# Expert layer of a cross-attention kernel: first tiles from three batches' tokens, routing of the fourth among the tiles, tiles past the 20th in branches

## The chip, the cores and the metric

One core of one Trainium2 chip runs the whole program as a single launch. The metric is device time in microseconds: the median over runs. The engines named below are PE (TensorE, matmuls), DVE (VectorE), ACT (ScalarE), POOL (GpSimd) and SP (SyncE, which only issues DMAs). Lines L... are those of the kernel before, unless the text says otherwise.

## The reference, cut to what matters

The input `x` is 4 batches x 512 tokens x 256 features, 2,048 tokens in all. Four layers follow each other, each adding to `x`:

```
def _L1_ffn_ref(x, W1, b1, W2, b2, Wr, br):          # D=256, H=1024, E=8, TOPK=2
    xf = x.reshape(-1, D)
    logits = xf @ Wr + br
    topv, _ = lax.top_k(logits, TOPK)
    masked = jnp.where(logits >= topv[:, 1:2], logits, -jnp.inf)
    weights = jax.nn.softmax(masked, axis=-1)
    h = gelu(jnp.einsum('td,edh->eth', xf, W1) + b1[:, None, :], approximate=False)
    expert_out = jnp.einsum('eth,ehd->etd', h, W2) + b2[:, None, :]
    return jnp.einsum('etd,te->td', expert_out, weights).reshape(B, S, D)

x = x + L0_xattn(...); x = x + L0_ffn(layernorm(x), ...)
x = x + L1_xattn(ctx, layernorm(x), ...); x = x + L1_ffn(layernorm(x), ...)
```

The last line's last term is the second expert layer, which the change is about. A token goes to the two experts with the largest logits, and to more only where logits tie. So 2,048 tokens make 4,096 rows of work, spread over eight experts as the router's choices fall. No expert has a capacity in this layer.

## The kernel before

The program runs four stages: attention 0 (to about 1710 us), the first expert layer (to about 1900), attention 1 (to 2676) and the second expert layer (to the end).

**How a token finds its expert.** The tensor `rows_x` in device memory has 2,048 places for each of the eight experts, 256 spare rows at the end, and in each row the 256 normalised features, the token's number and its eight routing weights (265 floats, 1,060 bytes). `clear_rows` (L334 to L345) fills it early in attention 0 with zeros and an out-of-range token number, by 32 DMAs of 530 KB and one of 265 KB on SP's queue. The exchanges of attention 0 (`swapped<-attn`, L700) are issued on SP behind them, and some on ACT.

`route2(b, ...)` (L347 to L473) routes a batch's tokens, in steps (it is a generator). It normalises four tiles of 128 tokens into `pay` (L354) and writes the token numbers behind them (L362); transposes them and multiplies by the router's matrix (L372); takes two experts by the two largest logits (L394 to L416); counts how many earlier tokens went to each expert (matmuls L432, L435) and so has each token's place; and scatters the rows of `pay` to those places with eight indirect DMAs on POOL (L446: four tiles, two experts). All of them write `rows_x`, so each waits for the one before. It ends by adding the second layer's bias to `x` (L459 to L470) and writing `x` to the output. `out` then holds everything but the expert products, which the tiles add to it.

**Where routing is done.** Attention 1 is a hand-written schedule in steps: for each batch four units (two halves of the features `o`, two halves of the tokens `f`) of 13 steps. `put(step, ...)` places a piece of work in a step, `spread` places a generator's pieces. Batch b-1 is routed during batch b (L1230: eight pieces, one per step). For batch 3 the units run with `f` outermost (L1034), so that the first half of its tokens is done after two units and is routed in the last two (L1251, L1252). The second half is routed after attention, ahead of the tiles (L1312). Within each engine the framework's planner places the instructions; it may move one ahead where its operands allow.

**The tiles.** From the counts a table (L1319 to L1362) is computed: expert by expert, as many tiles of 256 rows as its tokens fill; which expert's weights (`w_idx`) and which rows (`x_idx`) belong to tile i. There are always NG = 23 tiles (L52), the most that 4,096 rows over eight experts can need. A tile past the last real one reads the spare rows, whose token number is out of range, so its result is dropped. For tile i `fetch(i)` (L1364) gathers two blocks of 128 rows (L1368) and the expert's 2.1 MB of weights (L1378), by three indirect DMAs on POOL; `turned` (L1388) transposes the rows on PE (L1394) and copies them (L1395); `told` reads the token numbers and weights; `hidden` (L1409) is 32 matmuls (L1417 with gelu on ACT at L1425); `second` (L1433) is 32 more (L1436); `results` (L1495) multiplies by the routing weight on DVE (L1499) and adds to `out` by an accumulating scatter on POOL (L1500). Tile i+2 is fetched while tile i is computed, and the second product of tile i comes after the first of tile i+1. Row buffers are threefold, weights fourfold, results fivefold (`three`, `four`, `five`).

For ties a branch (L1457) computes the extra experts' share; its condition is loaded into a register, and it isn't taken where no logits tie.

Of the kernel before, what the change touches and what calls it, by code (L numbers as in the profile page):

```python
# [8 lines left out]
F32 = mybir.dt.float32  # L9
I32 = mybir.dt.int32  # L10
# [37 lines left out]

T = B * S
G = 256  # L50
GR = G // P
NG = (2 * T + E * (G - 1)) // G  # L52
ROWS = E * T
# [11 lines left out]
def xattn_ffn_twice(ctx: ExitStack, tc: tile.TileContext, a: dict, out: bass.AP):  # L65
# [79 lines left out]
    rows_x = dram.tile([ROWS + G, PAY], F32, name="rows_x")  # L145
# [176 lines left out]
    place2 = [const.tile([P, NX], I32, name=f"place2{k}") for k in range(2)]  # L322
# [11 lines left out]
    def clear_rows(empty):  # L334

        nc.gpsimd.memset(empty, 0.0)
        nc.gpsimd.memset(empty[:, :, D : D + 1], NOWHERE)
        n = ROWS // (4 * P)
        for i in range(n):
            nc.sync.dma_start(  # L340
                rows_x[i * 4 * P : (i + 1) * 4 * P, :].rearrange("(p r) d -> p r d", p=P), empty
            )
        nc.sync.dma_start(
            rows_x[ROWS:, :].rearrange("(p r) d -> p r d", p=P), empty[:, :GR, :]
        )  # L345

    def route2(b, two, psum, tag, first=0, n=NT):  # L347
# [90 lines left out]
        yield  # L438
        for k in range(2):
            off, place, at = small("off2"), wide("place"), place2[k][:, mine_b]  # L440
            nc.vector.tensor_tensor(place, hot[k], ps, ALU.mult)
            nc.vector.tensor_reduce(off, place, AX.X, ALU.add)
            nc.vector.scalar_tensor_tensor(off, chosen[k], float(T), off, ALU.mult, ALU.add)
            nc.vector.tensor_copy(at, off)
            for t in range(n):
                nc.gpsimd.indirect_dma_start(  # L446
                    out=rows_x[:, :],
                    out_offset=bass.IndirectOffsetOnAxis(ap=at[:, t : t + 1], axis=0),
                    in_=pay[:, t, :],
                    in_offset=None,  # L450
                    bounds_check=ROWS - 1,
                    oob_is_err=False,
                )

# [536 lines left out]
    with ExitStack() as st:  # L991
# [40 lines left out]
        for b in range(B):  # L1032
            order = [(o, f) for o in range(DC) for f in range(2)]
            if b == B - 1:  # L1034
                order = [(o, f) for f in range(2) for o in range(DC)]
            units += [(b, o, f) for o, f in order]
# [188 lines left out]
        for b in range(B):  # L1225
            s0 = per_batch * b
            if b:
                put(s0 - 10, lambda b=b: load_keys(b, 0))
                put(s0, lambda b=b: load_keys(b, 1))
                spread(s0 + 12, route2(b - 1, one, ps_s, "s"))  # L1230
# [20 lines left out]
        last_half = route2(B - 1, one, ps_s, "s", 0, NT // 2)  # L1251
        spread(per_batch * (B - 1) + 2 * NM + 12, last_half, 1, 8)  # L1252
# [49 lines left out]
    with ExitStack() as st:  # L1302
# [9 lines left out]
        for _ in route2(B - 1, two, ps_t, "t", NT // 2, NT // 2):  # L1312
            pass


        def bc(t, shape, at):
            return t.unsqueeze(at).to_broadcast(shape)

        count = one.tile([P, E], F32, name="count")  # L1319
        ps = ps_t.tile([P, E], F32, tag="t", name="ps_n")  # L1320
        nc.tensor.matmul(ps, lhsT=ones, rhs=taken2, start=True, stop=True)
        nc.vector.tensor_copy(count, ps)
        steps = one.tile([P, E, T // G], F32, name="steps")
        nc.vector.tensor_tensor(
            steps, bc(count, [P, E, T // G], 2), bc(full, [P, E, T // G], 1), ALU.is_gt
        )
        tiles = one.tile([P, E], F32, name="tiles")
        nc.vector.tensor_reduce(tiles, steps, AX.X, ALU.add)
        upto = one.tile([P, E], F32, name="upto")
        sums = one.tile([P, E, E], F32, name="sums")  # L1330
        nc.vector.tensor_tensor(sums, bc(tiles, [P, E, E], 1), notafter, ALU.mult)
        nc.vector.tensor_reduce(upto, sums, AX.X, ALU.add)
        past = one.tile([P, NG, E], F32, name="past")
        nc.vector.tensor_tensor(
            past, bc(number, [P, NG, E], 2), bc(upto, [P, NG, E], 1), ALU.is_ge
        )
        which = one.tile([P, NG], F32, name="which")
        nc.vector.tensor_reduce(which, past, AX.X, ALU.add)
        w_at = one.tile([P, NG], F32, name="w_at")
        w_idx = one.tile([P, NG], I32, name="w_idx")  # L1340
        nc.vector.tensor_scalar(w_at, which, float(E - 1), float(P), ALU.min, ALU.mult)
        nc.vector.tensor_scalar(w_at, w_at, lane[:, 0:1], None, ALU.add)
        nc.vector.tensor_copy(w_idx, w_at)

        spent = one.tile([P, NG, E], F32, name="spent")
        nc.vector.tensor_tensor(spent, past, bc(tiles, [P, NG, E], 1), ALU.mult)
        x_at = one.tile([P, NG], F32, name="x_at")
        nc.vector.tensor_reduce(x_at, spent, AX.X, ALU.add)
        nc.vector.tensor_tensor(x_at, number, x_at, ALU.subtract)
        held_ = one.tile([P, NG], F32, name="held_")  # L1350
        nc.vector.tensor_scalar(held_, which, float(E), None, ALU.is_lt)
        nc.vector.tensor_tensor(x_at, x_at, held_, ALU.mult)
        nc.vector.scalar_tensor_tensor(x_at, which, float(T // G), x_at, ALU.mult, ALU.add)
        nc.vector.tensor_scalar(x_at, x_at, float(G), lane[:, 0:1], ALU.mult, ALU.add)
        x_idx = one.tile([P, GR, NG], I32, name="x_idx")
        nc.vector.tensor_copy(x_idx[:, 0, :], x_at)
        for r in range(1, GR):
            nc.vector.tensor_scalar(x_at, x_at, float(P), None, ALU.add)
            nc.vector.tensor_copy(x_idx[:, r, :], x_at)
        mine = one.tile([P, NG, E], F32, name="mine2")  # L1360
        nc.vector.tensor_scalar(mine, past, -1.0, 1.0, ALU.mult, ALU.add)
        nc.vector.tensor_tensor(mine[:, :, 1:], mine[:, :, 1:], past[:, :, : E - 1], ALU.mult)  # L1362

        def fetch(i):  # L1364
            rows = []
            for r in range(GR):
                got = three.tile([P, PAY], F32, tag=f"rows{r}", name=f"rows{r}")
                nc.gpsimd.indirect_dma_start(  # L1368
                    out=got,
                    out_offset=None,  # L1370
                    in_=rows_x[:, :],
                    in_offset=bass.IndirectOffsetOnAxis(ap=x_idx[:, r, i : i + 1], axis=0),
                    bounds_check=ROWS + G - 1,
                    oob_is_err=False,
                )
                rows.append(got)
            w = four.tile([P, WIDE], F32, tag="w", name="w_e")
            nc.gpsimd.indirect_dma_start(  # L1378
                out=w,
                out_offset=None,  # L1380
                in_=a["wall"],
                in_offset=bass.IndirectOffsetOnAxis(ap=w_idx[:, i : i + 1], axis=0),
                bounds_check=E * P - 1,
                oob_is_err=False,
            )
            return w, rows
# [10 lines left out]

        def told(i, rows):

            to = five.tile([P, GR], I32, tag="to", name="to")  # L1400
            share = five.tile([P, GR], F32, tag="share", name="share")
            for r in range(GR):
                nc.vector.tensor_copy(to[:, r : r + 1], rows[r][:, D : D + 1])
                of = two.tile([P, E], F32, tag="told", name="told")
                nc.vector.tensor_tensor(of, rows[r][:, D + 1 :], mine[:, i, :], ALU.mult)
                nc.vector.tensor_reduce(share[:, r : r + 1], of, AX.X, ALU.add)
            return to, share
# [37 lines left out]
        fetched = [fetch(0), fetch(1)]  # L1445
# [3 lines left out]
        ps = ps_t.tile([P, NX], F32, tag="t", name="ps_x")  # L1449
        nc.tensor.matmul(ps, lhsT=ones, rhs=over, start=True, stop=True)  # L1450
        n_over = one.tile([P, 1], F32, name="n_over")
        nc.vector.tensor_reduce(n_over, ps, AX.X, ALU.add)
        n_over_i = one.tile([P, 1], I32, name="n_over_i")
        nc.vector.tensor_copy(n_over_i, n_over)
        ties = nc.values_load(n_over_i[0:1, 0:1], min_val=0, max_val=E * T)
        spare = st.enter_context(tc.tile_pool(name="d_spare", bufs=1))
        with tc.If(ties > 0):  # L1457
            for b in range(B):
                for t0 in range(0, NT, GR):
                    rows = []  # L1460
                    for r in range(GR):
                        j = b * NT + t0 + r
                        got = spare.tile([P, PAY], F32, tag=f"again{r}", name=f"again{r}")
                        nc.gpsimd.indirect_dma_start(
                            out=got,
                            out_offset=None,
                            in_=rows_x[:, :],
                            in_offset=bass.IndirectOffsetOnAxis(
                                ap=place2[0][:, j : j + 1], axis=0
                            ),  # L1470
                            bounds_check=ROWS + G - 1,
# [120 lines left out]
```

## Time and profile before

| what | us |
|---|---|
| median of 3 runs (3060.4 to 3063.5) | 3061.97 |
| the profiled execution | 3062.4 |
| its span, first to last instruction | 3060.7 |
| last update of `x` by attention 1 ends | 2676.7 |
| first hidden matmul of the tiles (L1417) | 2724.95 |
| last matmul of the tiles (L1436) ends | 3054.26 |
| last add to `out` issued (L1500) | 3055.09 |
| PE busy in the span | 2826.6 (92%) |
| mean granted clock of PE | 0.957 |

The span is what the profile shows; the execution's own time lies 1.7 us above it. In groups of instructions, a line reads: line, engine, operation, output<-input, shape, count, then busy time. In the timeline a line begins with the start and the duration, and a bracket at its end tells how long the engine was idle before and what released it. In a table of waits the numbers are total, times, longest. A cell of the windows is an engine's busy time with the number of its instructions.

### The profile page before, as it was taken

The page shows a single profiled execution, that of the slowest core. Times are in us where ns is not written, and L with a number is a line of the kernel's source. Part 1 is how long each engine was busy: PE and PEld are TensorE (multiplying, and loading weights), DVE is VectorE, ACT ScalarE, POOL GpSimd, SP SyncE. Part 2 cuts the span into 40 slices and gives each one's busy share as a digit, 9 for nine tenths or more (in the row PEclk, how much of TensorE's full clock was granted, in tenths as well). Part 3 has the DMA queues.
Part 4 walks back from the last instruction along what each step waited for, and adds up shares of the span by engine and source line. Part 5 has one row for each costly group of instructions (what it writes and reads, how often), then busy time and mean ns, then how long its engine had stood idle before and what let it go on. Part 6 is the DMA issues. An engine that isn't in the chain of part 4 may idle for free. (4 is left out here: it accounts for less than half of the span.)

```text
span 3060.7 us, 35871 instructions
## 1 busy us (share of the span) xinstructions
PE 2826.6 (92%) x13564; PEld 1885.8 (62%) x13564; DVE 1439.2 (47%) x2351; ACT 931.6 (30%) x1328; POOL 476.8 (16%) x347
## 2 busy tenths in 40 slices
PE   5899999999999999999997999599989897759999
PEld 2566666666666667676664666344545444448888
DVE  4365456544565444454443000577657566621111
ACT  2233234223342323323221211144334343412221
POOL 1000000100001000010001000333333333434442
PEclk9899999999999999999997999699999998969999
DMA  8543343343433433343333331300010100045562
GB/s 309 173 116 99 100 109 89 102 103 100 110 89 104 102 91 94 86 107 98 96 96 120 120 110 55 85 12 23 17 43 15 34 15 24 12 162 184 171 194 72
DMA packets 160942, 293.94 MB, mean 96 GB/s; under 512 B 42825, under 2 KB 78015, under 8 KB 157561
## 3 DMA queue, kind: packets, MB, share of 16 engines
q1 hardware_dynamic: 118280, 181.12, 21.3%
q0 software_dynamic: 17904, 74.77, 7.7%
q10 hardware_dynamic: 24576, 35.68, 4.5%
q8 instruction: 108, 1.77, 0.2%
q14 instruction: 74, 0.60, 0.1%
HBM read 100.24 MB, written 42.69 MB: 47 GB/s over the span
## 5 line engine op out<-in xcount | busy, mean ns | idle before, releaser
L687 DVE TENSOR_REDUCE top<-ps_s 128x1 f32<-128x2113 f32 x128 | 301.8, 2358 | 582.2 <-PE ps_s L679 576.6
L716 PE MATMUL ps_o<-pT,v 128*128 128x256 f32 x2176 | 521.6, 382 | 7.9 <-DVE pT L708 7.9
L679 PE MATMUL ps_s<-kT,qT 128*128 128x512 f32 (+1 forms) x1280 | 490.8, 528 | 15.2 <-ACT attn L693 14.7
L716 PEld LDWEIGHTS ps_o<-pT,v 128*128 128x128 f32 x2176 | 411.5, 192 | 125.1 <-issue 69.9
L679 PEld LDWEIGHTS ps_s<-kT,qT 128*128 128x128 f32 x1280 | 242.6, 191 | 265.7 <-issue 240.8
L693 ACT ACTIVATE attn<-ps_s,top 128x2113 f32<-128x2113 f32 x128 | 258.9, 2023 | 475.7 <-DVE top L687 411.2
L708 DVE STREAM_TRANSPOSE pT<-swapped 128x2176 f32<-128x2176 f32 x128 | 312.4, 2440 | 58.1 <-DMA swapped<-attn 48.2
L1080 DVE TENSOR_REDUCE tops<-ps_s 128x2 f32<-128x800 f32 (+1 forms) x256 | 243.0, 982 | 84.8 <-PE ps_s L1072 84.4
L1119 PE MATMUL ps_w<-asked,keyed 64*128 64x256 f32 (+1 forms) x1664 | 241.6, 422 | 41.0 <-DVE tops L1080 38.9
L629 PE MATMUL ps_k<-kvin,wkv 128*128 128x512 f32 (+1 forms) x640 | 262.1, 534 | 4.2 <-ACT kT L636 4.2
L1141 POOL TENSOR_TENSOR sum<-sum,pT 128x1024 f32<-128x1024 f32 x80 | 201.0, 2513 | 390.6 <-PE ps_o L1150 201.3
L662 PE MATMUL ps_v<-wkv,kvin 128*128 128x256 f32 x1088 | 253.5, 381 | 0.0
L1132 ACT ACTIVATE pT<-ps_w 128x1024 f32<-128x1024 f32 (+1 forms) x176 | 176.1, 1023 | 221.5 <-PE ps_w L1119 219.7
L1119 PEld LDWEIGHTS ps_w<-asked,keyed 64*128 64x128 f32 (+1 forms) x1664 | 156.0, 196 | 134.2 <-DVE tops L1080 74.4
L662 PEld LDWEIGHTS ps_v<-wkv,kvin 128*128 128x128 f32 x1088 | 204.9, 190 | 32.6 <-issue 3.3
L1072 PE MATMUL ps_s<-kT,qT 32*128 32x400 f32 (+1 forms) x1024 | 162.1, 588 | 30.1 <-DVE tops L1080 27.9
L1141 DVE TENSOR_TENSOR sum<-sum,pT 128x1024 f32<-128x1024 f32 x96 | 144.0, 1500 | 91.2 <-ACT pT L1132 78.0
L636 ACT ACTIVATE kT<-ps_k,bqk 128x512 f32<-128x512 f32 (+1 forms) x160 | 97.2, 620 | 268.2 <-PE ps_k L629 121.0
L629 PEld LDWEIGHTS ps_k<-kvin,wkv 128*128 128x128 f32 x640 | 116.5, 192 | 80.0 <-issue 67.1
L1417 PE MATMUL ps_h<-xT,w_e 128*128 128x256 f32 x736 | 164.7, 383 | 0.0
L1436 PE MATMUL ps_y<-w_e,hT 128*128 128x256 f32 x736 | 162.5, 379 | 0.0
L1417 PEld LDWEIGHTS ps_h<-xT,w_e 128*128 128x128 f32 x736 | 141.4, 192 | 19.6
(239 smaller groups left out, 2599.2 us busy)
## 6 DMA issues: line engine op xcount, KB each, us to landing
swapped<-attn SPq DMA_DIRECT2D x1536, 68.0 KB
swapped<-attn ACTq DMA_DIRECT2D x512, 68.0 KB
rows_x<-empty SPq DMA_DIRECT2D x32, 530.0 KB
w<-in_w_dram SPq DMA_DIRECT2D x16, 1024.0 KB
cT<-in_ctxT_dram SPq DMA_DIRECT2D x4, 1601.0 KB
keyed<-kT SPq DMA_DIRECT2D x32, 200.1 KB
ctx_b<-in_ctx_dram SPq DMA_DIRECT2D x4, 1536.0 KB
slot_x<-empty POOLq DMA_DIRECT2D x8, 512.0 KB
```

Source lines behind the costliest of these rows:

```text
L629: nc.tensor.matmul(ps[:, :n], lhsT=wkv[:, c, hs], rhs=flat_kvin[c][:, j0 : j0 + n], start=c == 0, stop=c == DC - 1,)
L662: nc.tensor.matmul(ps[:, k, :], lhsT=flat_kvin[c][:, j * P : (j + 1) * P], rhs=wkv[:, c, cols], start=c == 0, stop=c == DC - 1,)
L679: nc.tensor.matmul(flat[:, j0 : j0 + n], lhsT=qT[:, t * P : (t + 1) * P], rhs=kT[:, j0 : j0 + n], start=True, stop=True,)
L687: nc.vector.tensor_reduce(top, flat[:, :L], AX.X, ALU.max, negate=True)
L693: nc.scalar.activation(attn[:, :L], flat[:, :L], AF.Exp, bias=top, accum_out=total)
L708: nc.vector.transpose(pT[:, :, k * P : (k + 1) * P].rearrange("p c (a i) -> p a c i", a=4), swapped.rearrange("p a (c i) -> p a c i", i=32),)
L716: nc.tensor.matmul(ps, lhsT=v[:, j - parts[part][0], (h % 2) * DH0 : (h % 2 + 1) * DH0], rhs=pT[:, j, :], start=j == 0, stop=j == NB - 1,)
L1080: nc.vector.tensor_reduce(tops[u][:, t, 2 * pair : 2 * pair + 2, k], pss[pair][:, :, : hi - lo], AX.X, ALU.max,)
L1119: nc.tensor.matmul(ps[:r, s, pair * QH : (pair + 1) * QH], lhsT=keyed[o][64 * s : 64 * s + 64, pair, j * P : j * P + r], rhs=asked[u % 3][ ...
L1132: nc.scalar.activation(pT[:r], ps[:r], AF.Exp)
L1141: (nc.gpsimd if k else nc.vector).tensor_tensor(to, to, pT[:r], ALU.add)
L1417: nc.tensor.matmul(ps[:, f, :], lhsT=w[:, at : at + P], rhs=xT[:, c, :], start=c == 0, stop=c == DC - 1,)
```

## The change

`rows_x` is split. `rows_a` holds the first 256 places of each expert, as far as tokens of batches 0 to 2 fill them; `rows_b` holds 2,304 places for each expert, with every other row. Tokens of the first three batches are scattered to both tensors by 16 DMAs a batch, the index being out of range in the one that they don't belong to. Tokens of batch 3 go to `rows_b` alone (eight DMAs). Both tensors are cleared as `rows_x` was: 20,736 rows instead of 16,640.

Batch 3's units run in the same order as the others', and its routing, all four tiles, moves behind attention 1. There it is one generator with the table, of which three pieces are issued per tile. The tiles are now: one first tile for each expert, read from `rows_a` by plain DMAs on SP, weights too; 12 further tiles from `rows_b`, fetched on POOL with the table's indices; and tiles past these (up to 21 further ones) in nested branches, each with its own fetch and computation. Two counts are loaded into registers behind the 20 tiles. Routing pieces of batches 0 to 2 come every third step, 13 of them, instead of eight in consecutive steps. The block for ties, which changes too, is left out of the diff, as are the parts of the table and the functions that stay.

```diff
 T = B * S
 G = 256
 GR = G // P
-NG = (2 * T + E * (G - 1)) // G
-ROWS = E * T
+PLACES = T + G
+ROWS = E * PLACES
+NG = (2 * T - 2 * G + E * (G - 1)) // G
+SURE = 12
 PAY = D + 1 + E
...
-    rows_x = dram.tile([ROWS + G, PAY], F32, name="rows_x")
+    rows_a = dram.tile([E * G, PAY], F32, name="rows_a")
+    rows_b = dram.tile([ROWS + G, PAY], F32, name="rows_b")
...
-        n = ROWS // (4 * P)
-        for i in range(n):
-            nc.sync.dma_start(
-                rows_x[i * 4 * P : (i + 1) * 4 * P, :].rearrange("(p r) d -> p r d", p=P), empty
-            )
-        nc.sync.dma_start(
-            rows_x[ROWS:, :].rearrange("(p r) d -> p r d", p=P), empty[:, :GR, :]
-        )
+        for rows in (rows_a, rows_b):
+            n = rows.shape[0]
+            for i in range(0, n, 4 * P):
+                some = rows[i : min(i + 4 * P, n), :]
+                nc.sync.dma_start(
+                    some.rearrange("(p r) d -> p r d", p=P), empty[:, : some.shape[0] // P, :]
+                )
...
+        if b == B - 2:
+            nc.vector.tensor_copy(taken_a, taken2)
         for k in range(2):
-            off, place, at = small("off2"), wide("place"), place2[k][:, mine_b]
+            off, place, at, out_of = small("off2"), wide("place"), small("at2"), small("out_of")
             nc.vector.tensor_tensor(place, hot[k], ps, ALU.mult)
             nc.vector.tensor_reduce(off, place, AX.X, ALU.add)
-            nc.vector.scalar_tensor_tensor(off, chosen[k], float(T), off, ALU.mult, ALU.add)
-            nc.vector.tensor_copy(at, off)
-            for t in range(n):
-                nc.gpsimd.indirect_dma_start(
-                    out=rows_x[:, :],
-                    out_offset=bass.IndirectOffsetOnAxis(ap=at[:, t : t + 1], axis=0),
-                    in_=pay[:, t, :],
-                    in_offset=None,
-                    bounds_check=ROWS - 1,
-                    oob_is_err=False,
-                )
+            if b < B - 1:
+                for to, width, past in (
+                    (place_a, G, ALU.is_ge),
+                    (place_b, PLACES, ALU.is_lt),
+                ):
+                    nc.vector.tensor_scalar(out_of, off, float(G), NOWHERE, past, ALU.mult)
+                    nc.vector.tensor_tensor(out_of, out_of, off, ALU.add)
+                    nc.vector.scalar_tensor_tensor(
+                        at, chosen[k], float(width), out_of, ALU.mult, ALU.add
+                    )
+                    nc.vector.tensor_copy(to[k][:, mine_b], at)
+            else:
+                nc.vector.scalar_tensor_tensor(
+                    at, chosen[k], float(PLACES), off, ALU.mult, ALU.add
+                )
+                nc.vector.tensor_copy(place_b[k][:, mine_b], at)
+                nc.vector.memset(place_a[k][:, mine_b], int(NOWHERE))
+        yield
+        for rows, at in ((rows_a, place_a), (rows_b, place_b))[b == B - 1 :]:
+            for k in range(2):
+                for t in range(n):
+                    j = b * NT + first + t
+                    nc.gpsimd.indirect_dma_start(
+                        out=rows[:, :],
+                        out_offset=bass.IndirectOffsetOnAxis(ap=at[k][:, j : j + 1], axis=0),
+                        in_=pay[:, t, :],
+                        in_offset=None,
+                        bounds_check=E * G - 1 if rows is rows_a else ROWS - 1,
+                        oob_is_err=False,
+                    )
+                yield
...
-            if b == B - 1:
-                order = [(o, f) for f in range(2) for o in range(DC)]
...
-                spread(s0 + 12, route2(b - 1, one, ps_s, "s"))
+                spread(s0 + 12, route2(b - 1, one, ps_s, "s"), 3, 13)
...
-        last_half = route2(B - 1, one, ps_s, "s", 0, NT // 2)
-        spread(per_batch * (B - 1) + 2 * NM + 12, last_half, 1, 8)
...
-        for _ in route2(B - 1, two, ps_t, "t", NT // 2, NT // 2):
-            pass
...
+        def told(rows, share_of):
+            to = five.tile([P, GR], I32, tag="to", name="to")
+            share = five.tile([P, GR], F32, tag="share", name="share")
+            for r in range(GR):
+                nc.vector.tensor_copy(to[:, r : r + 1], rows[r][:, D : D + 1])
+                share_of(share[:, r : r + 1], rows[r][:, D + 1 :])
+            return rows, to, share
+        def first_tile(e):
             rows = []
             for r in range(GR):
                 got = three.tile([P, PAY], F32, tag=f"rows{r}", name=f"rows{r}")
-                nc.gpsimd.indirect_dma_start(
-                    out=got,
-                    out_offset=None,
-                    in_=rows_x[:, :],
-                    in_offset=bass.IndirectOffsetOnAxis(ap=x_idx[:, r, i : i + 1], axis=0),
-                    bounds_check=ROWS + G - 1,
-                    oob_is_err=False,
-                )
+                nc.sync.dma_start(got, rows_a[e * G + r * P : e * G + (r + 1) * P, :])
                 rows.append(got)
             w = four.tile([P, WIDE], F32, tag="w", name="w_e")
-            nc.gpsimd.indirect_dma_start(
-                out=w,
-                out_offset=None,
-                in_=a["wall"],
-                in_offset=bass.IndirectOffsetOnAxis(ap=w_idx[:, i : i + 1], axis=0),
-                bounds_check=E * P - 1,
-                oob_is_err=False,
-            )
-            return w, rows
+            nc.sync.dma_start(w, a["wall"][e * P : (e + 1) * P, :])
+            def share_of(to, weights):
+                nc.vector.tensor_copy(to, weights[:, e : e + 1])
+            return w, rows, share_of
...
+        def table():
...
+            skip = one.tile([P, E], F32, name="skip")
+            nc.vector.tensor_scalar(skip, count[:, 1, :], float(G), None, ALU.min)
+            rest = one.tile([P, E], F32, name="rest")
+            nc.vector.tensor_tensor(rest, count[:, 0, :], skip, ALU.subtract)
...
+            nc.vector.tensor_tensor(spent, mine, bc(skip, [P, NG, E], 1), ALU.mult)
+            nc.vector.tensor_reduce(held, spent, AX.X, ALU.add)
+            nc.vector.tensor_tensor(x_at, x_at, held, ALU.add)
+            nc.vector.scalar_tensor_tensor(x_at, which, float(PLACES), x_at, ALU.mult, ALU.add)
...
+        def further_tile(i):
...
+                    in_=rows_b[:, :],
+                    in_offset=bass.IndirectOffsetOnAxis(
+                        ap=state["x_idx"][:, r, i : i + 1], axis=0
+                    ),
...
+        def routing():
+            yield from route2(B - 1, two, ps_t, "t")
+            yield from table()
+        rest = routing()
+        fetched = [first_tile(0), first_tile(1)]
+        more = [lambda e=e: first_tile(e) for e in range(2, E)]
+        more += [lambda i=i: further_tile(i) for i in range(SURE)]
+        def ready(w, rows, share_of):
+            return (w, turned(rows), *told(rows, share_of)[1:])
+        last = None
+        next(rest)
+        here = ready(*fetched.pop(0))
+        for i in range(E + SURE):
+            w, xT, to, share = here
+            hT = hidden(w, xT)
+            for _ in range(3):
+                next(rest, None)
+            if more:
+                fetched.append(more.pop(0)())
+            if fetched:
+                here = ready(*fetched.pop(0))
+            if last:
+                results(*last)
+            last = (w, to, share, hT)
+        results(*last)
+        assert next(rest, None) is None
+        n_tiles = tc.nc.values_load(state["counts"][0:1, 0:1], min_val=0, max_val=NG)
+        ties = tc.nc.values_load(state["counts"][0:1, 1:2], min_val=0, max_val=E * T)
+        def beyond(i):
+            with tc.If(n_tiles > i):
+                w, xT, to, share = ready(*further_tile(i))
+                results(w, to, share, hidden(w, xT))
+                if i + 1 < NG:
+                    beyond(i + 1)
+        beyond(SURE)
```

## The prediction

> **What bounds the kernel now.** I read the 40 slices and the issue table of the page first, then a table of windows, the timeline around the end of attention 1, the waits of its last quarter, and the chain at the end. PE is busy 92% of the span, so I look for stretches in which it isn't.
>
> ```profile
> PE   5899999999999999999997999599989897759999
> ...
> rows_x<-empty SPq DMA_DIRECT2D x32, 530.0 KB
> ```
>
> In the slices, the first (clearing, loading) and those before the last four stand out. The windows, with PE, PEld, DVE, ACT and POOL busy, then granted clock, DMA share and GB/s:
>
> ```profile
> 30.00:90.00 60.00, 52.64 (x170) 29.79 (x169) 16.34 (x29) 18.49 (x29) 9.97 (x14) 0.94 0.91 347
> 2677.00:2725.00 48.00, 10.29 (x35) 7.21 (x36) 14.16 (x86) 2.07 (x4) 13.12 (x13) 0.50 0.45 164
> 2740.00:2984.00 244.00, 244.00 (x1168) 214.90 (x1167) 39.84 (x152) 57.80 (x139) 106.93 (x85) 1.00 0.58 179
> 3054.30:3060.70 6.40, 0.00 (x0) 0.00 (x0) 0.48 (x1) 0.00 (x0) 1.54 (x1) 0.72 0.01 0
> ```
>
> Three things: the clear keeps the DMA engines 91% busy until 90 us; between attention and the expert tiles PE works 10 of 48 us at half clock; the tiles leave PE no gap, so each costs its PE time. The gap, on POOL and PE:
>
> ```profile
> 2691.34 0.97 POOL L446 DMA_INDIRECT rows_x<-pay,place  x1 [1.80 <-DMA rows_x<-pay,place]
> ...
> 2705.42 0.99 POOL L446 DMA_INDIRECT rows_x<-pay,place  x1 [6.82 <-DMA rows_x<-pay,place]
> 2706.72 1.04 POOL L1378 DMA_INDIRECT w_e<-in_wall_dram,w_idx  x1 [0.30 <-issue]
> 2717.45 1.02 POOL L1368 DMA_INDIRECT rows<-rows_x,x_idx  x1 [9.69 <-DMA rows_x<-pay,place]
> ...
> 2720.30 0.45 PE L1394 MATMUL tp<-ident,rows 128*128 128x128 f32 x1 [29.07 <-DMA rows<-rows_x,x_idx]
> 2724.95 16.19 PE L1417 MATMUL ps_h<-xT,w_e 128*128 128x256 f32 x64
> ```
>
> Each scatter waits for the one before; a 2.1 MB weight gather between two stretches 2.8 us to 9 to 12; no row is gathered until the last lands. Waits in 2430 to 2680:
>
> ```profile
> PE ps_w L1119 <- DVE tops L1080: 20.7, 8, 10.1
> PE ps_n L1168 <- POOL sum L1141: 6.4, 1, 6.4
> ```
>
> The 10.1 stands behind a wait of DVE, in all of stage c:
>
> ```profile
> DVE pay L362 <- DMA rows_x<-pay,place: 21.8, 3, 9.5
> ```
>
> DVE may not overwrite the routed rows' buffer until their scatters have read it, and the row maxima are queued behind. The three stalls are 3.8, 9.5 and 8.5 us.
>
> **What the Trainium skill says.** "DMA: Bandwidth & Descriptors", section "Anatomy of one DMA — SWDGE (gpsimd) path", fits such a transfer as 2.0 us plus bytes over 436 GB/s: 6.8 us for 2.1 MB (estimate); the trace's 9 to 12 us include a scatter, so nothing contradicts it. The same page, section "SWDGE vs HWDGE vs iDMA", says SWDGE has one queue allocated; the scatters stuck behind weights agree. "TensorE: Matmul & The Clock Gate", Part 1, has an idle array run at half clock: the 0.50 above, and 16.19 us for 64 matmuls against 14.14 at full clock. "Runtime: NRT & Kernel Launch", section "Instruction fetch mechanics", warns that a taken branch to a target not prefetched stalls the engine. Here the skipped ties branch left the next instruction 2.7 us later on ACT and 6 on DVE, hidden in the gap.
>
> **The change part by part**, against the profiled span of 3060.7.
>
> (a) Clear. 2,048 + 18,688 = 20,736 rows instead of 16,640: 4,096 x 1,060 B = 4.34 MB more, over the 390 GB/s of the stretch 11.1 us. SP's first exchange `swapped` is queued behind it, and DVE waits 20.7 us for that and PE 7.0 behind, so no cover is left. +11.1 (8 if ACT's exchanges hide some, 14 if engines share badly).
>
> (b) Attention 1. Batches 0 to 2 issue 16 scatters, not 8, and some 12 more small DVE operations each (36 x 0.17 = 6 us). POOL's order alternates rows_a and rows_b, each waiting only for its own tensor's last: eight pairs at 2.9 (0.97 issue + 1.9 landing) take as long as eight scatters, if two issues (2 x 1.3) fit in a link, which they just do. The two pay waits 3.8 and 9.5 stay; I add 5 us for both. Batch 3 now has a pay buffer of its own pool, so the third wait goes: PE's 10.1. Its first half's four scatters leave POOL, so the sum before the closing isn't late: 6.4. Half a batch of PE routing (8 transposes, 16 matmuls) leaves: 2. What is late next is the ordinary wait for `tops`. -13.5 (-22 to 0).
>
> (c) Gap. Before: last update of x ends 2676.7, stream starts 2724.95: 48.3. Afterwards the first expert's rows are long in rows_a, a plain load on SP; its weights reuse attention's memory and start when x is done: 2.1 MB at 380 to 480 GB/s, 5.5, and 2 to land, some 2 for the semaphores and transposes, and half clock over the first tile 2: 12 (10 to 20). -36.3. The routing's norm and logits (10 us in the trace) lie beside this load.
>
> (d) Routing of batch 3 in the stream. Its PE work, 16 logits matmuls, counts, transposes and bias, some 5 us at full clock, is now between tiles; before it was in the gap. Rows_b's scatters and the first adds are interleaved on POOL; SP has the write of out[3], which waits for the early adds, and the count loads ahead of the weights of tiles 6 and 7. DVE's cast for tile 6 takes a buffer that waits for tile 1's add and stands ahead of the copy that PE's bias needs. The trace shows neither; a stall of nothing if the adds run early, 20 if a tile and its weights slip. I take 6. +11 (+5 to +25).
>
> (e) Tiles. Counting the router's choices on the reference's own inputs: the experts get 200 375 342 772 902 432 636 437 tokens, of which 162 230 255 622 649 322 457 375 in batches 0 to 2. A first tile holds up to 256 of the latter; what is left, 38 145 87 516 646 176 380 181, makes 1 1 1 3 3 1 2 1 = 13 further tiles. So 8 + 12 in the stream, one in a branch. 23 tiles took 2724.95 to 3054.26, 329.3: 14.25 each and 1.6 at the start. 20: 286.6. -42.7 (exact unless a matmul changes).
>
> (f) End. Before: 6.4 from the last matmul. Now, after it: multiply and last add 2.9; loading two counts 1.2 (0.5 each in the trace); the branch, falling through, 0 to 3; two row gathers and one of weights at 1.3 of issue, and 7 to 8 of landing: hidden layer at +16 to 18. Nothing overlaps: 9 us at half clock, 8 for the second, multiply and add 3; then the jumps over the next branch and the ties branch, 0 to 6 each, and the drain. 44 (38 to 55): +37.6. So the one real tile past the 20th gives back nearly three streamed ones.
>
> Sum: 11.1 - 13.5 - 36.3 + 11 - 42.7 + 37.6 = -32.8. Span 3027.9; the profiled execution's 3062.4 becomes 3029.6; its 0.4 over the median of 3061.97 makes **3029**.
>
> **Rivals.**
> 1. Nothing runs in a branch. Expert 4's rest is 516, four over two tiles; rounding in the router could move a few tokens, but not likely four at the threshold. For it: how thin the margin is. (f) falls to some 3: 3029 - 35 = 2994.
> 2. The stream starves early. POOL carries scatters, adds and gathers in one queue, weights of 2.1 MB stretch scatters to 9 us in the trace, and the table needs all of batch 3 first; tile 8 must have its rows by some 8 x 14.25 = 114 us after the start. For: eight scatters at 9 are 72 us, plus the table. Against: SP now loads the weights, a different queue. One and a half tiles lost at 14.25: +21, 3050.
> 3. Slower: the 16 scatters run one after another. Then a batch takes 16 x 3.5 = 56 us rather than 28; DVE's pay wait and POOL's sums grow by 28 for each of three batches, 84, of which some 24 are covered by what POOL idles: +60, to 3089. It decides from +33. For: DVE already waited 9.5 us for eight, and the two issues only just fit a link. Against: the two tensors are independent, and the third pay wait is gone.
> 4. The clear is hidden: the exchange isn't what PE lacks but one of several waits. 3018; the 7.0 of PE behind it speaks against.
>
> **How the numbers follow.** Forecast with 4 taken in: 0.63, own range 3014 to 3044. Rival 1: 0.09. Rival 2: 0.19, 3044 to 3058. Rival 3: 0.09. The range reaches 3004 (attention and gap at their best) to 3052 (most of rival 2), leaving out rival 3, most of 1 and the top of 2, about 2 in 10. A measurement of this kernel tells 0.2%, 6 us, from no change: faster is the forecast, rival 1 and nearly all of 2, 0.88; same 0.04, between 2 and 3; slower 0.08.
>
> **What would show it.** First exchange near 101 us; no pay wait and no late sum in attention's last batch, two pay waits of 5 to 15 before; some 12 us from the last x update to the first hidden matmul; 20 tiles at 14.25 with 10 to 15 us more over the first ten; PE idle some 17 us before a last tile at half clock; nothing but drains after. Wrong if the pay waits double (rival 3), if PE waits for weights or rows among tiles 6 to 9 (rival 2), or if no tile follows the stream (rival 1).

## The result and the profile after

| | us |
|---|---|
| before, median of 5 runs (3056.52 to 3065.49) | 3061.97 |
| changed, median of 5 runs (3071.42 to 3078.07) | 3072.33 |
| ratio changed to before | 1.0035, 95% interval 1.0021 to 1.0048 |
| profiled execution of the changed kernel, and its span | 3071.42, 3069.6 |

The change made the kernel some 10 us slower; 33 us less was forecast. Measured a second time, beside e10 to e12 (e9 below), the ratio was 1.0040 (1.0028 to 1.0053). All ratios below are to the kernel before on the same chip, so a difference of 0.001 between two of them is 3 us.

Line numbers are now those of the changed kernel, except where the kernel before is named or a run has an edit that shifts them. Windows of the changed kernel, in the columns of the windows before (PE, PEld, DVE, ACT and POOL busy, granted clock, DMA share, GB/s):

```profile
90.00:109.00 19.00, 10.68 (x42) 7.52 (x40) 0.00 (x0) 2.74 (x6) 0.00 (x0) 0.84 1.01 378
2704.00:2714.00 10.00, 6.51 (x28) 5.72 (x29) 4.80 (x32) 2.07 (x3) 0.00 (x0) 0.50 0.93 360
2758.50:2784.40 25.90, 10.17 (x35) 7.67 (x33) 3.44 (x12) 0.84 (x2) 6.05 (x5) 0.63 0.21 53
2784.40:3024.60 240.20, 240.18 (x1139) 211.07 (x1138) 40.34 (x150) 53.75 (x128) 91.92 (x71) 1.00 0.51 152
3024.60:3069.60 45.00, 17.18 (x68) 14.03 (x68) 2.92 (x10) 3.36 (x8) 8.81 (x7) 0.73 0.23 63
```

The clear now fills the DMA engines until after 100 us, with DVE idle throughout 90 to 109. The gap between attention and tiles is 10 us, no longer 48. Among the first tiles there is a hole of 26 us in which PE works 10; the rest of the stream has none. The end is 45 us long. In the spans, stage by stage:

| step of the prediction | forecast | measured | from |
|---|---|---|---|
| (a) clear | +11.1 | +13.0 | a query product of attention 0 that began at 161.23 before and at 174.18 after |
| (b) attention 1 | -13.5 | +13.9 | last update of x ends 2676.7, then 2703.6; less (a) |
| (c) gap | -36.3 | -37.8 | first hidden matmul 10.5 us after that update |
| (d) routing in the stream | +11 | +23.8 | stream 2714.16 to 3024.59 is 310.4; less 286.6 |
| (e) three tiles fewer | -42.7 | -42.7 | from 2800 to 3020 PE has 1,049 matmuls, 68 a tile, in 220.0 us: 14.26 a tile, as before; what tiles take beyond that is in (d) |
| (f) end | +37.6 | +38.6 | 45.0 against 6.4 |
| sum | -32.8 | +8.8 | |

Four steps came out within 2 us. Attention 1 missed by 27, the routing in the stream by 13. The timeline of PE in attention 1, then the waits of DVE from 2160 to 2710 us:

```profile
2289.37 2.93 PE L1145 MATMUL ps_w<-asked,keyed 64*128 64x256 f32 x12 [18.85 <-DVE tops L1106]
...
2485.58 2.93 PE L1145 MATMUL ps_w<-asked,keyed 64*128 64x256 f32 x12 [17.42 <-DVE tops L1106]
```

```profile
DVE pay L368 <- DMA rows_b<-pay,place_b: 37.7, 2, 19.7
```

The third pay wait has gone, as forecast. The two that stayed are 19.7 and 18.0 us, where they were 3.8 and 9.5, and PE stands behind both (18.85 and 17.42 above).

In the tiles, DVE's timeline and then PE's show the other miss:

```profile
2774.97 0.21 DVE L1341 CAST to<-rows 128x1 int32<-128x1 f32 x2 [22.32 <-DMA out_dram<-y,to]
2775.10 0.67 DVE L489 COPY wbT<-tp_w 8x512 f32<-8x512 f32 x1
```

```profile
2775.82 3.78 PE L494 MATMUL ps_b<-b,wbT 8*128 8x256 f32 x8 [15.73 <-DVE wbT L489]
```

The cast of tile 6's token numbers takes the buffer `to` that tile 1 used, five tiles before, and waits for tile 1's add; the copy behind it is what PE needs. The bias products then take 3.78 us, twice what they take in e4: the granted clock is 0.50 from 2775.5 to 2779.8 here, and 1.00 around the same products in e4.

### The profile page after: what moved, and what is told of

It is laid out like the page before. It is cut to its first block, busy times and chain, and to the rows that moved or that the text cites. A ratio compares the mean times of both kernels' runs of the same rounds, so it can differ in the third digit from the quotient of the medians.

```text
span 3069.6 us, 35581 instructions
## 1 busy us (share of the span) xinstructions
PE 2803.5 (91%) x13426; PEld 1862.9 (61%) x13426; DVE 1433.0 (47%) x2324; ACT 923.1 (30%) x1307; POOL 462.4 (15%) x337
## 5 line engine op out<-in xcount | busy, mean ns | idle before, releaser
L707 PE MATMUL ps_s<-kT,qT 128*128 128x512 f32 (+1 forms) x1280 | 490.4, 528 | 25.9 <-ACT attn L721 25.5
L1378 PE MATMUL ps_h<-xT,w_e 128*128 128x256 f32 x672 | 151.9, 385 | 6.2 <-DMA w_e<-in_wall_dram,w_idx 6.2
L1397 PE MATMUL ps_y<-w_e,hT 128*128 128x256 f32 x672 | 151.3, 383 | 0.0
L1386 ACT ACTIVATE hT<-ps_h,w_e 128x256 f32<-128x256 f32 x168 | 70.4, 471 | 262.0 <-issue 173.4
```

The costliest lines, as they stand in the source:

```text
L707: nc.tensor.matmul(flat[:, j0 : j0 + n], lhsT=qT[:, t * P : (t + 1) * P], rhs=kT[:, j0 : j0 + n], start=True, stop=True,)
```

## The experiments

Times of attention 1 in this table run from the transposes (`tp_o`) that close one batch's last unit to those that close the next one's, in PE's timeline of each run. "Pay waits" are DVE's waits for scatters before it may write the token numbers. Each row is one profiled execution, and the two of the changed kernel (changed, e9) differ by 2 to 5 us a batch: smaller differences between rows say nothing.

| run | ratio (95%) | batch 1 | batch 2 | batch 3 | pay waits |
|---|---|---|---|---|---|
| before | 1 | 188.4 | 183.4 | 146.2 | 3.8, 9.5, 8.5 |
| changed | 1.0035 (1.0021 to 1.0048) | 198.6 | 193.2 | 140.0 | 19.7, 18.0 |
| e9 changed again | 1.0040 (1.0028 to 1.0053) | 201.3 | 191.4 | 144.8 | 22.3, 17.6 |
| e1 numbers later | 0.9948 (0.9931 to 0.9964) | 183.3 | 179.8 | 144.2 | none |
| e5 one scatter | 0.9955 (0.9940 to 0.9971) | 191.8 | 186.7 | 135.8 | 18.8, 15.0 |
| e6 before, numbers later | 0.9938 (0.9921 to 0.9955) | 184.1 | 179.4 | 143.2 | none |
| e10 every step | 0.9965 (0.9953 to 0.9976) | 196.4 | 194.3 | 127.6 | 13.8, 13.4 |
| e11 before, spaced | 1.0058 (1.0038 to 1.0077) | 193.0 | 187.1 | 154.0 | 17.8, 16.3, 15.8 |

**e1: the token numbers depend on the batch.**

```diff
         mv, rs = ln_stats(two, xb, n)
+        zero = two.tile([P, n], F32, tag="zero", name="zero")
+        nc.vector.tensor_scalar(zero, rs, 0.0, None, ALU.mult)
...
-                pay[:, t, D : D + 1], lane, float((b * NT + first + t) * P), None, ALU.add
+                pay[:, t, D : D + 1], lane, float((b * NT + first + t) * P), zero[:, t : t + 1], ALU.add, ALU.add
```

> Edit: the token numbers written behind the routed rows depend on the batch's own norm (a zero made from it is added), so that the planner cannot move this write ahead to where it waits for the last batch's 16 scatters. Theory A (that hoisted write, 18.0 and 19.7 us of DVE waiting in batches 1 and 2, is what attention 1 lost): both waits go, PE's waits for the row maxima of 18.9 and 17.4 us go with them, 25 to 36 us off the changed kernel's 3072, so 3036 to 3047. Theory B (the doubled scatters hold POOL for 30 us a batch, and the partial sums behind them would be late in any case): PE waits for the sums instead, and at most 10 us go, 3062 or more.

Measured 3050.38, a ratio 0.0087 under the changed kernel's: 27 us. PE's waits for the maxima in attention 1 (from 2160 us on), in the kernel before, the changed kernel and e1:

```profile
PE ps_w L1119 <- DVE tops L1080: 30.8, 16, 10.1
...
PE ps_w L1145 <- DVE tops L1106: 62.2, 19, 18.9
...
PE ps_w L1147 <- DVE tops L1108: 27.1, 17, 7.2
```

So theory A: the write needs nothing but a constant, the planner puts it far ahead of its use, and it then holds up DVE for a buffer whose next rows come only some 90 us later (in the changed kernel the numbers are written at 2285 and the features beside them at 2376). Sums on POOL did not become late instead: PE has no wait for one of 1.8 us or more in e1.

**e2: fewer places.**

```diff
-PLACES = T + G
+PLACES = T - G
```

> Edit: rows_b has 1,792 places for each expert instead of 2,304, so 16,640 rows are cleared in all, as before the change. An expert with more tokens than places would lose some; with these inputs none has over 902. Theory A (the clear delays the first exchange, and everything after, by what it is longer): the first exchange is issued at 90 us as before, 13 us off, 3059. Theory B (part of the 13 us is the split into more queued transfers or other changes in the start): 5 us or less, 3067 or more.

Measured 3061.92, ratio 0.9988 (0.9972 to 1.0004), 14 us under the changed kernel, for theory A (13). The query product of (a) is back at 161.14 us, and DVE's wait for the first exchange, in 85 to 130 us, at its length of before (20.5, with 31.5 in the changed kernel):

```profile
DVE pT L736 <- DMA swapped<-attn: 24.7, 2, 20.5
```

**e3: thirteen further tiles in the stream.**

```diff
-SURE = 12
+SURE = 13
```

> Edit: 13 further tiles in the stream instead of 12, so that the branches hold no real tile with these inputs. Theory A (the tile in the branch runs with no overlap and costs 45 - 10 us at the end, the streamed one 14.25): 20 to 23 us off, 3050. Theory B (the register loads, the jump over the branches and the drain are most of the 45 us): the end stays over 25 us from the last matmul, and the kernel gains under 10 us, 3062 or more.

Measured 3057.91, ratio 0.9974 (0.9965 to 0.9983), 19 us under the changed kernel, just short of theory A (20 to 23). The window behind its last matmul:

```profile
3037.40:3049.90 12.50, 0.03 (x1) 0.00 (x0) 0.48 (x1) 0.00 (x0) 1.54 (x1) 0.62 0.17 21
```

That is all that loads, jumps and drain cost: 12.5 us, 6.1 more than the drain of the kernel before. The other 32.5 of the changed kernel's 45 are the tile itself, as its timeline on PE shows:

```profile
3033.46 0.45 PE L1366 MATMUL tp<-ident,rows 128*128 128x128 f32 x1 [8.88 <-DMA rows<-rows_b,x_idx]
...
3041.76 8.92 PE L1378 MATMUL ps_h<-xT,w_e 128*128 128x256 f32 x32 [6.16 <-DMA w_e<-in_wall_dram,w_idx]
3050.52 7.07 PE L1397 MATMUL ps_y<-w_e,hT 128*128 128x256 f32 x32
```

Entering the branch cost next to nothing (POOL's times are in the last section); waiting for rows and weights with nothing to do meanwhile cost 15 us (the rows are gathered only behind POOL's last add of the stream, at 3030), and the first product ran for 8.92 instead of 7.07.

**e4: ten index buffers.**

```diff
+        ten = st.enter_context(tc.tile_pool(name="d_ten", bufs=10))
...
-            to = five.tile([P, GR], I32, tag="to", name="to")
-            share = five.tile([P, GR], F32, tag="share", name="share")
+            to = ten.tile([P, GR], I32, tag="to", name="to")
+            share = ten.tile([P, GR], F32, tag="share", name="share")
```

> Edit: the token numbers and weights that told writes (to, share) have ten buffers instead of five; they are a few bytes each. Theory A (DVE's cast into the fifth buffer waits 22.3 us for an early add, with the copy wbT behind it, and PE for that copy): PE's 15.7 us at ps_b go, 15 us off, 3057. Theory B (the adds are late because batch 3's scatters and 2.1 MB weights share the DMA engines, so the y buffers, the row buffers or the weights of tiles 6 to 8 come late next): PE waits 10 us or more elsewhere between 2740 and 2800, and under 6 us go.

Measured 3062.62, ratio 0.9982 (0.9969 to 0.9996), 16 us under the changed kernel, for theory A (15). PE goes through the bias without a wait, and the next late thing is a result that DVE has not yet read:

```profile
2765.78 1.99 PE L494 MATMUL ps_b<-b,wbT 8*128 8x256 f32 x8
...
2787.75 3.72 PE L1398 MATMUL ps_y<-w_e,hT 128*128 128x256 f32 x16 [1.84 <-DVE y L1424]
```

Its stream is 2719.85 to 3016.50, 296.7 us instead of 310.4: what is left of (d) is 10 us, about half of it waits like the last line's (4.7 us in two).

**e5: eight scatters.** The number of DMAs is changed, and the rest left as it is. This kernel leaves out the rows past an expert's 256th place, so its output is not the layer's.

```diff
-        for rows, at in ((rows_a, place_a), (rows_b, place_b))[b == B - 1 :]:
+        for rows, at in ((rows_a, place_a), (rows_b, place_b))[b == B - 1 :][:1]:
```

> Edit: batches 0 to 2 scatter to rows_a alone, eight DMAs a batch as before the change. Left out: their rows past an expert's 256th place, which the further tiles then read as cleared rows. Theory A (the doubling makes the pay wait long): DVE's pay waits fall from 37.7 us to 13 to 20 (they were 3.8 and 9.5 in the kernel before, for the same two batches), and 18 to 25 us go, 3047 to 3054. Theory B (the write of the token numbers stands earlier in DVE's order than before, so that it waits long for any scatters): the two waits stay over 28 us, and under 10 us go.

The waits went B's way, the time A's. In the waits of DVE:

```profile
DVE pay L368 <- DMA rows_a<-pay,place_a: 33.7, 2, 18.8
```

Eight scatters make DVE wait nearly as long as sixteen, and 24 us went all the same (0.9955), 7 us from each of batches 1 and 2 and 4 from batch 3. So the doubled scatters do cost, some 17 us in attention 1, of which only 4 are this wait's length. That the wait is still long with eight must come from where the write stands.

**e6: the kernel before, with e1's edit.**

> Edit: the kernel before, with the token numbers depending on the batch's norm as in e1. Theory A (each of the three waits of 3.8, 9.5 and 8.5 us costs PE what its own wait shows, 2.9, 8.6 and 10.1): 15 to 22 us under the kernel before, 3040 to 3047; so what the change added to this wait was some 15 us, and what it lost by keeping the write where it was is some 35. Theory B (PE only moves its waiting to other places, since POOL's and DVE's work in those batches is the same): under 8 us.

Measured 3049.06, ratio 0.9938: 19 us, theory A. Beside e1 its batches are equal within about 1 us (table). For batches 1 and 2, in which the two kernels differ in the scatters, their places and the spacing, this says: once the write is out of the way, 16 scatters with spaced pieces cost what eight without spacing did. For batch 3 it says less, since the kernel before also routes half of batch 3 in it.

**e10 and e11: the spacing.** What e5 left open is why DVE is at the write so early. In the changed kernel's trace six DVE instructions lie between the last place of a batch and the next batch's numbers, in both batches; in the kernel before, 18 and 14. In time, the first scatter on POOL and the write on DVE, in the kernel before and then in the changed one:

```profile
2202.66 1.03 POOL L446 DMA_INDIRECT rows_x<-pay,place  x1 [6.11 <-DVE off L442]
2230.54 0.34 DVE L362 TENSOR_SCALAR pay<-lane 128x1 f32<-128x1 f32 x4 [3.82 <-DMA rows_x<-pay,place]
...
2253.71 1.03 POOL L473 DMA_INDIRECT rows_a<-pay,place_a  x1 [13.34 <-DVE out_of L457]
2285.13 0.15 DVE L368 TENSOR_SCALAR pay<-lane 128x1 f32<-128x1 f32 x1 [19.67 <-DMA rows_b<-pay,place_b]
```

DVE arrives where its idle time begins: 24.1 us behind the first scatter before (at 2226.72) and 11.8 now (at 2265.46). In the next batch it is 16.4 and 11.6. The edits take the spacing of the routing pieces out of the changed kernel (e10, shown), and put it into the kernel before (e11, the reverse at the same place):

```diff
-                spread(s0 + 12, route2(b - 1, one, ps_s, "s"), 3, 13)
+                spread(s0 + 12, route2(b - 1, one, ps_s, "s"), 1, 13)
```

> Edit: in the changed kernel the routing pieces of batches 0 to 2 come in consecutive steps, as before the change, instead of every third. In the built order of DVE's instructions the write of the token numbers then stands 12 to 13 instructions behind the last place (15 and 14 in the kernel before, 6 in the changed one). Theory A (the spacing moved this write ahead and so made DVE reach it 12 us sooner): the two pay waits fall from 37.7 us to 15 to 24, and 10 to 20 us go, 3052 to 3062. Theory B (the length of the 16 scatters decides): the waits stay over 30 us and under 6 us go.

> Edit: in the kernel before, with its eight scatters a batch, the routing pieces come every third step. This puts the write of the token numbers 6 instructions behind the last place for batches 1 and 2 and 11 for batch 3. Theory A (as in e10): pay waits of 15 to 20 us in batches 1 and 2 instead of 3.8 and 9.5, and 12 to 22 us more than the kernel before, 3074 to 3088. Theory B: waits as before, within 6 us of it.

e10: 3057.79, ratio 0.9965, against 1.0040 for the unedited kernel (e9) on the same chip: 23 us, more than theory A's 10 to 20. e11: 3082.13, ratio 1.0058: 18 us slower than the kernel before, by the spacing alone. First DVE's timeline in e10 and PE's wait behind it, then DVE's waits in e11:

```profile
2247.36 0.34 DVE L368 TENSOR_SCALAR pay<-lane 128x1 f32<-128x1 f32 x4 [13.75 <-DMA rows_b<-pay,place_b]
...
2443.11 0.34 DVE L368 TENSOR_SCALAR pay<-lane 128x1 f32<-128x1 f32 x4 [13.40 <-DMA rows_b<-pay,place_b]
...
PE ps_v L917 <- DVE tops L1106: 25.1, 2, 12.9
```

```profile
DVE pay L362 <- DMA rows_x<-pay,place: 50.0, 3, 17.8
```

With eight scatters and no other part of the change, the waits in e11 are 17.8, 16.3 and 15.8, nearly as long as in the changed kernel, and DVE arrives 10.9 to 12.0 us behind the first scatter. So the spacing is enough to make the write early and the wait long.

It isn't all of it. In e10 the waits fell to 27.2 in all, between the two theories, with DVE arriving 15.1 and 16.4 us behind the first scatter. And the time that e10 gained was not at these waits: batches 1 and 2 took 390.7 us, where the changed kernel took 391.8 and 392.7 (e9). PE waited less for DVE there, but its own work took longer: 339 us instead of 329, at a granted clock of 0.91 instead of 0.92 and 0.93. The gain is in batch 3, which no theory had: 127.6 us against 140.0 and 144.8 (e9), and 18.6 under the kernel before. No pay wait stands in batch 3, and e1, without any, has 144.2, so what the spacing cost there isn't the write. Spaced, the routing of batch 2 reaches into the last units of batch 3; that this is the reason is likely, and not tested by itself.

**e7: the clear in steps.**

```diff
-                nc.sync.dma_start(
+                yield lambda some=some: nc.sync.dma_start(
...
-        clear_rows(empty)
+        clears = list(clear_rows(empty))
...
+        for k, f in enumerate(clears):
+            later[min(k // PER, 18)].append(f)
```

`PER` is 3.

> Edit: the 41 clearing DMAs are issued three by three in the first 14 of the 128 steps of attention 0, between the exchanges, instead of all ahead of the first. Theory A (only the queue ahead of the first exchange costs): DVE's wait of 31.5 us for the first exchange falls to 5 or less, and PE's 18.7 behind it goes, 20 to 27 us off the changed kernel, 3045 to 3052. Theory B (the same bytes are only taken from later exchanges, each of which then waits for three clears, 4 us): the later exchanges take the time back, and under 8 us go.

Measured 3062.79, ratio 0.9982 (0.9971 to 0.9993), 16 us under the changed kernel, between the two theories; but its profiled execution, the slowest of its 11, has a span of 3070.0, that of an unedited one. In that profile the first part is 18 us earlier (156.18 against 174.18 for the query product of (a)) and the last such product only 6 (1522.4 against 1528.9). The waits of 85 to 200 us:

```profile
DVE top L716 <- PE ps_s L708: 55.5, 10, 10.7
...
ACT kT L665 <- DMA swapped<-attn: 11.2, 4, 3.4
```

The waits for exchanges are now short and several, and PE has become the one that DVE waits for. What took back 12 of the 18 us later on isn't shown. How much of the gain lasts stays open: 16 us by the ratio, none by the one profile.

**e8 and e12: the edits together.** e8 has e1, e3, e4 and e7; e12 is e8 without e7.

> Edit: token numbers later (e1), 13 further tiles in the stream (e3), ten index buffers (e4) and the clear in steps (e7) together. Theory A (the losses lie in four different places and add up: by the ratios 27 + 19 + 16 us, and 20 to 27 for the clear): 80 to 90 us off the changed kernel, 2983 to 2993, well under the kernel before. Theory B (what is taken from one place is waited for in the next, in attention 1 above all): 3010 or more.

> Edit: e8 without the clear in steps, that is token numbers later, 13 further tiles in the stream, ten index buffers. Theory A (the clear in steps gives back at the exchanges of attention 0 what it gains at the first, as e7's profile shows with 18 us gained by 160 us and 6 left by 1520): within 8 us of e8, 3005 to 3013. Theory B (it was worth its 13 us or more there): 3017 or more.

e8: 3004.59, ratio 0.9803 (0.9783 to 0.9823), 71 us under the changed kernel and 2% under the one before; that is between its two theories. e12: 3012.68, ratio 0.9830 (0.9809 to 0.9851), for theory A at its upper edge. The three edits of e12 gain 64 us on e9, and singly they gave 27 + 19 + 16 = 62: they add up. The clear in steps adds 8 us more by the ratios, with intervals that overlap, so it isn't shown that it adds anything here. e8's end and stream, by windows:

```profile
2675.00:2988.40 313.40, 307.52 (x1444) 268.67 (x1442) 55.08 (x229) 71.80 (x170) 113.30 (x88) 0.98 0.53 164
2988.40:3000.70 12.30, 0.00 (x0) 0.00 (x0) 0.45 (x1) 0.00 (x0) 1.54 (x1) 0.67 0.17 22
```

Twenty-one tiles in 313 us, 14.9 each with the routing of batch 3 among them, and an end of 12.3.

**e9: the changed kernel again.**

> The changed kernel itself, unedited, on the chip of the runs e10 to e12, so that they have it beside them. Theory A (its first measurement, a ratio of 1.0035, holds): 1.002 to 1.005. Theory B (the differences of e1 to e8 by profile, smaller than by ratio by some 7 us on average, are the truer ones): 0.999 to 1.002.

1.0040 (1.0028 to 1.0053), theory A. The runs of one kernel differ by up to 23 us (3050.91 to 3073.47 in e2), and a profiled execution is one of them; that is why the sizes of whole edits above are taken from ratios.

## Why the prediction was wrong

**(a)** was right: 13.0 for 11.1, and e2 gives it back. The rival of a hidden clear falls.

**(b)** is the step that failed: -13.5 was forecast and +13.9 measured. It failed in two terms, and the diff's other line there, pieces every third step and 13 of them, was priced in neither.

The first term is the sentence "The two pay waits 3.8 and 9.5 stay; I add 5 us for both". They grew by 24 us together, and batches 1 and 2 took 20 us more instead of 5. With the wait out of the way (e1) that loss is gone. A wait's length is the release less the arrival, and both ends moved: 17 of the 24 us are an earlier arrival of DVE behind the first scatter (from 24.1 and 16.4 us to 11.8 and 11.6), 7 a later release (from 27.9 and 25.9 us to 31.4 and 29.5). I had left the arrival where it was; e11 shows that the spacing alone moves it. What batches 1 and 2 took together says what each cause cost, in us:

| batches 1 and 2 | eight scatters | sixteen scatters |
|---|---|---|
| pieces in consecutive steps | 371.8 (before) | 390.7 (e10) |
| pieces every third step | 380.1 (e11), 378.5 (e5) | 391.8 (changed), 392.7 (e9) |
| write tied to the batch | 363.5 (e6) | 363.1 (e1) |

e5 and e11 differ by all the rest of the change and agree within 2 us. So the spacing costs 7 to 8 us there with eight scatters and nothing that stands out of the noise with sixteen; the second eight scatters cost 12 to 19; and with the write tied neither costs anything. I had judged the scatters right in length (sixteen in pairs took 26.9 to 29.2 us from first to last issue, eight had taken 23.3 to 27.3), but not in what they cost through this write. Why that is more than the wait's growth stays open. The slower rival put the loss in this very wait, and its sign, pay waits that double, came true; its cause, scatters one after another at 56 us a batch, did not.

The second term is the 18.5 us for batch 3, of which the changed kernel got 6. Without the spacing (e10) it is 18.6, so near the forecast partly by luck, as two profiles of one kernel differ by more (4.8 in this batch, changed and e9). The spacing took 12 us or more of this term, and that is the part of attention's miss that e10 gives back. No run joins e10's edit to e1's; batch 3 alone suggests some 16 us more there (144.2 less 127.6, an estimate).

**(c)** and **(e)** were right to 1.5 us: the plain loads of `rows_a` do close the gap.

**(d)** had the right mechanism and a term too small: a stall of 6 for the cast's buffer, where 15.7 was measured. I had 20 as the upper end. Tile 1's adds stood on POOL behind the last scatters, one of which waited 7.1 us for the one before while weights were loading, as had tile 0's second add for its first (7.4); I had taken the adds to be early. The rival of a starving stream (PE waiting for weights or rows among tiles 6 to 9) did not happen: after 2784 PE has no idle time.

**(f)** was right: 45.0 for 44. One real tile past the twentieth did run in the branch, and the rival without one falls. e3 shows that loads and jumps cost 6 us, and the tile in the branch the rest.

## What to carry to other kernels

A cheap write with no inputs of its own is free to be planned anywhere, and if its buffer is still being read it blocks a whole engine there; look for such writes whenever the schedule around them changes, and tie them to the data that they go with. When a wait "stays", ask for both its ends: a change that only spaces work out can move the waiter's arrival by more than it moves the release. But don't take the length of a wait for its price: e10 shortened the two waits by 10 us and gained in another batch. A tile outside the pipeline cost more than two inside it here (32.5 us against 14.25), so size the pipelined part for what the inputs really bring.

## What the runs showed of the hardware

Two chains of dependent scatters to different tensors, issued in turn on POOL, take little longer than one: 16 in 26.9 to 29.2 us from first to last issue in the changed kernel, where one chain of eight took 23.0 to 26.5 (e5). The price of entering a branch that falls through didn't show on POOL: its last add of the stream is issued at 3028.53 and takes 1.55 us, and its first gather in the branch follows 0.30 us later, at 3030.39, the same idle time as between the gathers. A scatter of batch 3 that had 2.9 us to the next in a quiet stretch (2762.45 to 2765.34) had 8.1 (2751.53 to 2759.66) where a plain weight load was issued on SP's queue at 2751.94; in e9 the same place shows 7.8 (2757.42 to 2765.21, the load at 2757.51). The other queue didn't shield it. For the gather of 2.1 MB the Trainium skill ("DMA: Bandwidth & Descriptors", "Anatomy of one DMA — SWDGE (gpsimd) path") gives 6.8 us by its fit, an estimate; in the branch, with nothing beside it but two small gathers, 8.65 us passed from the start of its issue (1.01 us of it) to the matmul that used it, and the measured time is the one to count with.
